# Loads and stores of whole activations cut by blocks of 128 rows rather than by groups of 32 partitions, in a two-layer graph network kernel

## The chip, the cores and the metric

The kernel runs on one core of one Trainium2 chip. Its time is the device time of one execution in microseconds (us); the median of three runs is what counts.

## The reference

There are B = 32 graphs of N = 512 nodes with F = 512 features, all in 32-bit floats. Two layers run one after the other, each on a normalized, rectified copy of the activations x:

```python
def reference(x, adj, nodemask, L0_gnn_W, L1_gnn_Wqk, L1_gnn_Wv):
    # layer 0
    h = jnp.maximum(_layernorm(x, axis=-1), 0.0)
    deg = jnp.sum(adj, axis=-1, keepdims=True)
    agg = jnp.einsum('bij,bjf->bif', adj, h) / jnp.maximum(deg, EPS)
    cat = jnp.concatenate([h, agg], axis=2)
    x = x + jax.nn.relu(jnp.einsum('bnf,of->bno', cat, L0_gnn_W))
    # layer 1
    h = jnp.maximum(_layernorm(x, axis=-1), 0.0)
    q, k = jnp.split(h @ L1_gnn_Wqk, 2, axis=-1)
    v = h @ L1_gnn_Wv
    agg = jnp.einsum('bij,bjd->bid', adj, k * mask[:, :, None])
    w = inv_scale * mask * jnp.einsum('bid,bid->bi', q, agg)
    return x + jax.nn.softmax(w, axis=1)[:, :, None] * v
```

(The two layers are written out in one function here; `mask` is nodemask, all ones in the data given, `inv_scale` is 1/sqrt(512), `EPS` 1e-6.)

## The kernel before

One graph is one batch of the loop (`for i in range(1, B)`, L1071 and after; batch 0 is in `start()`). Four matrix products are made for each batch, and each is cut into 2 by 2 blocks and made with seven block products instead of eight (`product`, L112, whose instructions all carry the line of `block_product`, L103). They run on TensorE in a fixed order: `layer1_tv(i - 1)` (tiles ptv, L470), `layer1_u(i)` (pp_u, pr_u, pq_u), `layer0_y(i + 1)` (pp_y and so on), `layer0_out(i + 1)` (pp_o and so on, fourteen block products). So the work of neighbouring batches is interleaved.

The order on every engine is written out by hand (`tc.manual_schedule`). While a product runs, a `Plan` says after which of its block products each other step is issued; `run` (L165) carries it out. So every engine's queue has a fixed order, and an instruction that waits holds up what stands behind it on the same engine. Nearly all DMAs are issued from SyncE (SP); GpSimd issues the ones that add dx onto the result (`add_x1`, L694), and ScalarE issues a few at the start and at the end.

Rows of a graph are laid out in SBUF in a permuted way. A row number is read as q, c, r with Q = 4 values of q, C = 4 values of c and R = 32 values of r, in that order, `row = 128 q + 32 c + r`. Row (q, c, r) stands in partition `32 q + r`, in chunk c of the free dimension. A tile [128, 4, 512] holds a graph's 512 rows of 512 floats, 2 KB each, in this way. This serves the transposition: the tile is written to a scratch buffer in DRAM (dhT, daT, dh1T; L309, L347, L382), read back by `exchange` (L206; tiles shT, saT, sh1T, 512-byte pieces), and turned in 32 by 32 blocks by VectorE (`turn`, L281).

These transfers go between DRAM and tiles in the permuted layout:

- `half_rows` (L202) loads half of a graph, two of the four chunks, into a tile of the pool "n" (two buffers, shared by both uses): x for the first normalization (`FrontH.load`, tile n; "late" for batch 1), and adj (`FrontA.load`, tile a). At the start it loads x of batch 0 into xu from two queues.
- `load_rows` (L193) loads a whole graph: x a second time for the residual sum (`load_x`, L232, tile xu, two buffers), and once the weight Wv (tile wvN).
- `store` (L714) writes half of a finished graph from tile tv, and `store_block` (L708) a quarter of the last one from tile out, alternating between the queues of SP and ScalarE.

All of them go through `by_rows` (L188): it makes four views of the DRAM side, one for each q, each with r outermost (32), then c, then the 512 floats. Each of these moves to or from 32 partitions. From the second pass of the main loop on they are placed so: the half loads of adj at step 12 of layer0_out and step 1 of layer1_tv, those of x at step 6 of layer1_u and step 0 of layer0_y, `load_x` at step 1 of layer0_y, and the stores at steps 9 and 11 of layer0_out. Between them SP issues the unchanged transfers: the scratch writes and reads above, dx (a copy of x after layer 0, 1 MB, L371), and seven tiles w of weights for each batch (`Stream.load`, L415, four buffers).

Of the kernel before, what the change touches and what calls it, by code (L numbers as in the profile page):

```python
# [22 lines left out]
def kernel(  # L23
# [11 lines left out]
    nc = tc.nc  # L35
    B, N, F = x.shape
    C = N // P
    H = F // 2
    Q = 4
    R = 32  # L40
# [144 lines left out]
        def at(self, n, f, *args):  # L185
            self.setdefault(n, []).append(lambda: f(*args))

    def by_rows(src):  # L188

        t = src.rearrange("(q c r) f -> q r c f", q=Q, c=C)  # L190
        return [t[q] for q in range(Q)]

    def load_rows(t, src):  # L193
        for q, rows in enumerate(by_rows(src)):
            nc.sync.dma_start(out=t[q * R:(q + 1) * R, :, :], in_=rows)

    def half_tile(name):
        return big.tile([P, 2, 512], F32, tag="n", bufs=2, name=name)
# [1 line left out]
    one_queue, two_queues = (nc.sync, nc.sync), (nc.sync, nc.scalar)  # L200

    def half_rows(t, src, h, queues=one_queue):  # L202
        for q, rows in enumerate(by_rows(src)):
            queues[q % 2].dma_start(out=t[q * R:(q + 1) * R, :, :], in_=rows[:, 2 * h:2 * h + 2, :])

    def exchange(src, name, t=None, queues=one_queue):  # L206

# [24 lines left out]
    def load_x(b):  # L232
        room_x(b)
        load_rows(X[b], x[b])
# [55 lines left out]
    class FrontH:  # L290
# [8 lines left out]
        def load(self, h, t=None):  # L299
            self.n[h] = half_tile(f"n_{self.b}_{h}") if t is None else t  # L300
            half_rows(self.n[h], x[self.b], h)
# [15 lines left out]
    class FrontA:  # L317
# [9 lines left out]
        def load(self, h):  # L327
            self.n[h] = half_tile(f"a_{self.b}_{h}")
            half_rows(self.n[h], adj[self.b], h)
# [298 lines left out]
    class Post:  # L628
# [77 lines left out]
                )  # L706

        def store_block(self, r, c):  # L708
            for q, dst in enumerate(by_rows(out[self.b])):
                (nc.scalar if q % 2 else nc.sync).dma_start(  # L710
                    out=dst[:, 2 * r:2 * r + 2, ts(c, H)], in_=self.o[q * R:(q + 1) * R, 2 * r:2 * r + 2, ts(c, H)]
                )

        def store(self, h):  # L714
            v = self.half(h).rearrange("p (c f) -> p c f", c=2)
            for q, dst in enumerate(by_rows(out[self.b])):
                nc.sync.dma_start(out=dst[:, 2 * h:2 * h + 2, :], in_=v[q * R:(q + 1) * R])


    wide = const.tile([P, 14, 2, H], F32, name="wide")  # L720
# [57 lines left out]
    def start():  # L778
# [24 lines left out]
        for h in range(2):  # L803
            half_rows(X[0][:, 2 * h:2 * h + 2, :], x[0], h, two_queues)
# [81 lines left out]
        nc.sync.dma_start(out=mask_sb, in_=nodemask)  # L886
        wvN = xu_tile("wvN").rearrange("p (c f) -> p c f", c=C)
        load_rows(wvN, wv)
        r2, l0 = right_sums(of(w2R)), left_sums(of(h0))

# [177 lines left out]
    with tc.manual_schedule(engines=engines):  # L1068
        weights, mvR = start()
        post = None  # L1070
        for i in range(1, B):  # L1071
            more, last = i + 1 < B, i + 1 == B
            f = F1[i] = FrontH1(i)
# [240 lines left out]
```

## Time and profile before

| | |
|---|---|
| median of 3 runs (lowest to highest) | 2264.93 us (2263.68 to 2269.67) |
| the profiled execution | 2263.74 us |
| span of its trace, first to last instruction | 2262.0 us |
| granted TensorE clock in it | 1.000 |
| HBM read, written | 293.93 MB, 167.51 MB |

One execution is profiled. "Busy" is the time in which an engine has an instruction running. The page gives busy times by engine, the span in 40 slices (busy tenths; for DMA the mean share of the core's 16 DMA engines, and GB/s), the DMA queues with the time that their packets took as a share of 16 engines, and the chain of work that ended last. The DMA list gives, for each line of the program that issues transfers, how many, how large, and how long from issue to landing (the median). The changed ones and their main neighbours, in the kernel before:

| transfer | issues | KB each | us to landing |
|---|---|---|---|
| a<-in_adj_dram | 256 | 128 | 3.0 |
| n<-in_x_dram | 240 | 128 | 3.7 |
| late<-in_x_dram | 8 | 128 | 8.3 |
| xu<-in_x_dram (load_x) | 124 | 256 | 5.4 |
| xu<-in_x_dram (start, 4 on SP, 4 on ScalarE) | 8 | 128 | 4.7 |
| wvN<-in_L_gnn_Wv_dram | 4 | 256 | 6.0 |
| out_dram<-tv | 248 | 128 | 3.4 |
| out_dram<-out (8 on SP, 8 on ScalarE) | 16 | 64 | 1.7 and 2.0 |
| w<-dw (unchanged) | 217 | 256 | 4.2 |
| dh1T<-h1m, sh1T<-dh1T (unchanged) | 124, 256 | 256, 128 | 3.2, 3.4 |
| dhT<-n, shT<-dhT (unchanged) | 120, 248 | 256, 128 | 2.7, 6.0 |
| daT<-a, saT<-daT (unchanged) | 124, 240 | 256, 128 | 3.0, 3.3 |
| tv<-dx, from GpSimd (unchanged) | 62 | 512 | 8.6 |

### The profile page before, as it was taken

Reading aid. Unit: us, or ns where it says so; the run is one execution under the profiler, and the core shown is the slowest. Engines: PE = TensorE matmul, PEld = TensorE weight load, DVE = VectorE, ACT = ScalarE, POOL = GpSimd, SP = SyncE. Lnnn points to the kernel's source line nnn. Section 1 sums busy time; section 2 is a strip of 40 time slices with the busy share of each in tenths; the row PEclk is TensorE's granted clock in tenths of the full one; section 3 lists DMA queues with packets and bytes.
Section 4 is the critical chain, followed back from the end, with each engine's and each line's share of the span. In section 5 each row is a group of like instructions: output and inputs, shape, how many; then the busy total and the mean of one; then the engine's idle time right before and its main releaser. Section 6 shows DMA issues by size and latency. Waiting matters only on the chain.

```text
span 2262.0 us, 32862 instructions
## 1 busy us (share of the span) xinstructions
PE 2253.7 (100%) x10526; PEld 1981.3 (88%) x10526; DVE 1913.5 (85%) x3778; ACT 1024.9 (45%) x1895; POOL 175.6 (8%) x261
## 2 busy tenths in 40 slices
PE   9999999999999999999999999999999999999999
PEld 7888888888888888888888888888888888888888
DVE  7988888888888888888888888888888888888776
ACT  4454443445434544434454344543444443445323
POOL 0010000000000000000000000000000000000000
PEclk9999999999999999999999999999999999999999
DMA  9988787888877887877878788888778777887644
GB/s 205 252 233 246 208 208 193 205 222 219 209 200 192 212 227 204 207 198 201 233 207 209 198 199 218 221 205 203 194 211 228 203 208 193 205 231 209 156 120 108
DMA packets 409997, 463.69 MB, mean 205 GB/s; under 512 B 38208, under 2 KB 271680, under 8 KB 405600
## 3 DMA queue, kind: packets, MB, share of 16 engines
q1 hardware_dynamic: 396608, 426.46, 69.3%
q0 software_dynamic: 8928, 32.51, 8.8%
q10 hardware_dynamic: 4288, 2.62, 0.6%
q8 instruction: 83, 1.36, 0.3%
q14 instruction: 90, 0.74, 0.1%
HBM read 293.93 MB, written 167.51 MB: 204 GB/s over the span
## 4 chain that ended last, share of the span: by engine, by line
PE 98%; DMA 1%; SPq 0%; ACT 0%; issue 0%; DVE 0%; DVEq 0%
PE ptv L470 28%; PE pp_o L103 19%; PE pp_y L103 10%; PE pp_u L103 10%; PE pq_o L103 9%; PE pq_y L103 5%; PE pq_u L103 5%; PE pr_o L103 5%; PE pr_y L103 2%; PE pr_u L103 2%; PE pw L521 1%; DMA mv<-in_L_gnn_Wqk_dram 0%; PE pp_v L103 0%; PE pp_t L103 0%; DMA w<-dw 0%; DMA xu<-in_x_dram 0%
## 5 line engine op out<-in xcount | busy, mean ns | idle before, releaser
L470 PE MATMUL ptv<-mv,h1T 128*128 128x256 f32 x2842 | 618.4, 379 | 0.0
L470 PEld LDWEIGHTS ptv<-mv,h1T 128*128 128x128 f32 x2842 | 539.9, 190 | 73.7 <-DVE xu L449 0.4
L74 DVE TENSOR_TENSOR tv<-tv 128x256 f32<-128x256 f32 (+1 forms) x645 | 322.0, 511 | 13.2 <-ACT tv L80 1.5
L80 ACT ACTIVATE tv<-ptv 128x512 f32<-128x512 f32 (+1 forms) x360 | 185.0, 541 | 262.9 <-PE ptv L470 261.9
L103 PE MATMUL pp_u<-h1m,aT 128*128 128x256 f32 x1024 | 241.9, 379 | 0.0
L103 PE MATMUL pp_y<-wide 128*128 128x256 f32 x992 | 234.4, 379 | 0.7 <-ACT y L80 0.7
L103 PE MATMUL pp_o<-y,aT 128*128 128x256 f32 x992 | 234.3, 379 | 0.0
L103 PE MATMUL pp_o<-w,wide 128*128 128x256 f32 x960 | 226.8, 379 | 0.0
L103 PEld LDWEIGHTS pp_u<-h1m,aT 128*128 128x128 f32 x1024 | 194.5, 190 | 26.4
L103 PEld LDWEIGHTS pp_y<-wide 128*128 128x128 f32 x992 | 188.3, 190 | 26.6 <-ACT y L80 1.1
L103 PEld LDWEIGHTS pp_o<-y,aT 128*128 128x128 f32 x992 | 188.4, 190 | 25.6
L103 PEld LDWEIGHTS pp_o<-w,wide 128*128 128x128 f32 x960 | 182.4, 190 | 24.8
L80 ACT ACTIVATE o<-pp_o 128x512 f32<-128x512 f32 x96 | 57.3, 597 | 300.1 <-PE pp_o L103 300.1
L80 ACT ACTIVATE y<-pp_y 128x512 f32<-128x512 f32 x124 | 74.0, 597 | 234.0 <-PE pp_y L103 234.0
L74 DVE TENSOR_TENSOR tv<-ptv,tv 128x512 f32<-128x512 f32 x240 | 139.9, 615 | 43.2 <-PE ptv L470 39.6
L80 ACT ACTIVATE xu<-pp_u 128x512 f32<-128x512 f32 x127 | 75.8, 597 | 193.6 <-PE pp_u L103 193.6
L77 DVE TENSOR_TENSOR h1T<-h1T 128x512 f32<-128x512 f32 (+1 forms) x183 | 158.3, 879 | 1.2
L251 POOL TENSOR_TENSOR rstd<-rstd,mhalf 128x2 f32<-128x2 f32 (+1 forms) x97 | 79.8, 823 | 642.5 <-DVE rstd L250 642.5
L103 PE MATMUL pq_u<-h1m,aT 128*128 128x256 f32 x512 | 121.0, 379 | 0.0
L74 DVE TENSOR_TENSOR tv<-ptv,m_tv 128x512 f32<-128x512 f32 (+1 forms) x120 | 72.1, 623 | 56.6 <-PE ptv L470 55.4
L103 PE MATMUL pq_y<-wide 128*128 128x256 f32 x496 | 117.3, 379 | 0.0
L103 PE MATMUL pq_o<-y,aT 128*128 128x256 f32 x496 | 117.2, 379 | 0.0
(173 smaller groups left out, 3354.7 us busy)
## 6 DMA issues: line engine op xcount, KB each, us to landing
w<-dw SPq DMA_DIRECT2D x217, 256.0 KB, 4.2
a<-in_adj_dram SPq DMA_DIRECT2D x256, 128.0 KB, 3.0
dx<-xu SPq DMA_DIRECT2D x32, 1024.0 KB, 5.0
sh1T<-dh1T SPq DMA_DIRECT2D x256, 128.0 KB, 3.4
shT<-dhT SPq DMA_DIRECT2D x248, 128.0 KB, 6.0
daT<-a SPq DMA_DIRECT2D x124, 256.0 KB, 3.0
xu<-in_x_dram SPq DMA_DIRECT2D x124, 256.0 KB, 5.4
dh1T<-h1m SPq DMA_DIRECT2D x124, 256.0 KB, 3.2
```

Source lines behind the costliest of these rows:

```text
L74: (on or nc.vector).tensor_tensor(o, a, b, op=ALU.add)
L77: (on or nc.vector).tensor_tensor(o, a, b, op=ALU.subtract)
L80: nc.scalar.activation(o, i, AF.Copy)
L103: nc.tensor.matmul(p[:, rc, :], lt[:, LEFT[k], dk, ts(rc, P)], right[:, dk, :], start=first and rc == 0 and dk == 0, stop=True, skip_group ...
L251: nc.gpsimd.tensor_tensor(rstd[:, a:b], rstd[:, a:b], mhalf[:, a:b], op=ALU.pow)
L470: nc.tensor.matmul(banks[n][:, :, ts(i, P)], left[:, LEFT[k], LEFT_IN[j], :], mvR[:, RIGHT[k], RIGHT[j], :, :], start=first and i == 0, st ...
L521: nc.tensor.matmul(banks[n][:, ts(i, P)], left[:, LEFT[k], LEFT_IN[j], :], mvR[:, RIGHT[k], RIGHT[j], which, :], start=first and i == 0, s ...
```

## The change

The four views of a DRAM tensor are cut by chunk c rather than by q. One transfer then moves one chunk, [128 partitions, 512 floats], between all 128 partitions and the DRAM rows (q, r) of this c: four blocks of 32 rows, 64 KB each, 256 KB apart. On the SBUF side its access pattern is partitions (128), then floats; on the DRAM side it is q (4), then r (32), then floats. A half load or a store of half a graph becomes two transfers of 256 KB where it was four of 128 KB; a load of a whole graph stays four of 256 KB. `four` returns its argument. The sequence of steps is the same on every engine; no compute instruction changes.

```diff
-    def by_rows(src):
-
-        t = src.rearrange("(q c r) f -> q r c f", q=Q, c=C)
-        return [t[q] for q in range(Q)]
+    def by_chunk(src):
+
+        t = src.rearrange("(q c r) f -> c q r f", q=Q, c=C)
+        return [t[c] for c in range(C)]
+
+    def four(v):
+        return v
 
     def load_rows(t, src):
-        for q, rows in enumerate(by_rows(src)):
-            nc.sync.dma_start(out=t[q * R:(q + 1) * R, :, :], in_=rows)
+        for c, rows in enumerate(by_chunk(src)):
+            nc.sync.dma_start(out=four(t[:, c, :]), in_=rows)
...
     def half_rows(t, src, h, queues=one_queue):
-        for q, rows in enumerate(by_rows(src)):
-            queues[q % 2].dma_start(out=t[q * R:(q + 1) * R, :, :], in_=rows[:, 2 * h:2 * h + 2, :])
+        for c, rows in enumerate(by_chunk(src)[2 * h:2 * h + 2]):
+            queues[c].dma_start(out=four(t[:, c, :]), in_=rows)
...
         def store_block(self, r, c):
-            for q, dst in enumerate(by_rows(out[self.b])):
-                (nc.scalar if q % 2 else nc.sync).dma_start(
-                    out=dst[:, 2 * r:2 * r + 2, ts(c, H)], in_=self.o[q * R:(q + 1) * R, 2 * r:2 * r + 2, ts(c, H)]
+            for a, dst in enumerate(by_chunk(out[self.b])[2 * r:2 * r + 2]):
+                (nc.scalar if a else nc.sync).dma_start(
+                    out=dst[:, :, ts(c, H)], in_=four(self.o[:, 2 * r + a, ts(c, H)])
                 )
 
         def store(self, h):
             v = self.half(h).rearrange("p (c f) -> p c f", c=2)
-            for q, dst in enumerate(by_rows(out[self.b])):
-                nc.sync.dma_start(out=dst[:, 2 * h:2 * h + 2, :], in_=v[q * R:(q + 1) * R])
+            for c, dst in enumerate(by_chunk(out[self.b])[2 * h:2 * h + 2]):
+                nc.sync.dma_start(out=dst, in_=four(v[:, c, :]))
```

## The prediction, made before the changed kernel was run

> **What bounds the kernel now.** I read the page from the top: busy shares, slices, DMA queues, chain.
>
> ```profile
> PE 2253.7 (100%) x10526; PEld 1981.3 (88%) x10526; DVE 1913.5 (85%) x3778; ACT 1024.9 (45%) x1895; POOL 175.6 (8%) x261
> ...
> DMA  9988787888877887877878788888778777887644
> GB/s 205 252 233 246 208 208 193 205 222 219 209 200 192 212 227 204 207 198 201 233 207 209 198 199 218 221 205 203 194 211 228 203 208 193 205 231 209 156 120 108
> DMA packets 409997, 463.69 MB, mean 205 GB/s; under 512 B 38208, under 2 KB 271680, under 8 KB 405600
> ...
> q1 hardware_dynamic: 396608, 426.46, 69.3%
> q0 software_dynamic: 8928, 32.51, 8.8%
> ...
> PE 98%; DMA 1%; SPq 0%; ACT 0%; issue 0%; DVE 0%; DVEq 0%
> ```
>
> TensorE sets the end: 2253.7 of 2262.0 us, and 98% of the chain. Only 8.3 us of the span have PE idle, so that is about the most a better transfer can win. But the DMA engines are no idle bystander: the queues' shares add up to 69.3 + 8.8 + 0.6 + 0.3 + 0.1 = 79.1% of sixteen engines. There is cover for a fifth more DMA work, if it is spread evenly, and not for more.
>
> Next the chain in order of time gives the beat of one batch, and the timeline of SP's queue shows where the changed transfers stand in it.
>
> ```profile
> 1086.94 21.15 PE ptv L470 x98
> ...
> 1132.27 3.45 PE pp_o L103 x16
> ...
> 1156.44 3.67 PE ptv L470 x17
> ```
> ```profile
> 1117.64 4.94 SPq L204 DMA_DIRECT2D n<-in_x_dram  x8
> 1122.68 1.79 SPq L195 DMA_DIRECT2D xu<-in_x_dram  x4
> 1125.61 1.79 SPq L212 DMA_DIRECT2D shT<-dhT  x4
> 1134.03 3.79 SPq L415 DMA_DIRECT2D w<-dw  x2
> ...
> 1145.32 1.74 SPq L717 DMA_DIRECT2D out_dram<-tv  x4
> ```
>
> One batch takes 1156.44 - 1086.94 = 69.50 us. In it SP issues, in one order, the four changed megabytes (half loads L204 of adj and of x, load L195 of x, stores L717) among the unchanged ones.
>
> Last, the stretches table (columns: stretch, length, busy time of each engine, clock, DMA share, GB/s) in two stretches each of two batches: the first and third lie in `w<-dw`, which fills 128 partitions, the others in `xu<-in_x_dram`, 32 partitions to a transfer.
>
> ```profile
> 619.00:621.00 2.00, 2.00 (x11) 1.76 (x10) 1.97 (x4) 1.25 (x3) 0.00 (x0) 1.00 1.02 376
> 637.00:639.00 2.00, 2.00 (x11) 1.77 (x10) 1.75 (x2) 0.09 (x1) 0.00 (x0) 1.00 1.04 255
> 688.50:690.50 2.00, 2.00 (x11) 1.75 (x10) 1.97 (x4) 1.25 (x3) 0.00 (x0) 1.00 1.02 380
> 706.50:708.50 2.00, 2.00 (x11) 1.77 (x10) 1.75 (x2) 0.09 (x1) 0.00 (x0) 1.00 1.01 253
> ```
>
> With all engines taken, 128-partition transfers move 376/16/1.02 = 23.0 GB/s an engine, 32-partition ones 255/16/1.04 = 15.3. This is what the change could win.
>
> **Part 1: fewer, wider transfers.** By the list of DMA issues the changed ones are a 256, n 240, xu 124 and 8, late 8, wvN 4, out 248 and 16: 904 issues, 134.2 MB, or 4.19 MB a batch. After it there are 516 (half loads and stores halve, load_x keeps four). SP spends 1.74/4 = 0.435 us on an issue, so 388 x 0.435 = 169 us of SP are saved, worth 0: SP is not on the chain (0%), and its long waits are on PE and ACT. No compute instruction is added or moved. A chunk's consumer now waits for one transfer instead of for four quarters; that is worth 0 too, because PE already runs without a gap.
>
> **Part 2: the packets.** They stay 2 KB. If all sixteen engines still share each transfer, the 4.19 MB cost 4.19/16/23.0 = 11.4 us an engine instead of 17.1: 5.7 us a batch less DMA, hidden behind PE.
>
> **Part 3: how a transfer is dealt out.** Before, the outermost count is 32 or 128 on both sides of every transfer. Now SBUF has 128 partitions, but DRAM is written as q (4) by r (32) by f: its outermost count is four. No row of the trace has such a transfer, so I bound: it is shared by sixteen engines (as in the `w<-dw` rows, whose share of 1.02 is of sixteen engines), or by four, one for each q block, and then whether these are the same four each time is open as well. I take four, always the same: the diff changes just this count, equal shares cut along it can't be more than four, and I see nothing that would rotate them.
>
> [...]
>
> **The sum for four engines**, per batch, on the four:
> - changed transfers: 4.19/4 = 1.05 MB an engine. At 23.0 GB/s 45.6 us, at 15.3 68.5. I take 45.6: the destination fills 128 partitions as in `w<-dw`.
> - the rest, still on all sixteen: 79.1% of 2262 over 32 batches is 55.9 us; less the changed ones' present 4.19/16/15.3 = 17.1 leaves 38.8. If the rest too ran at 23.0, its (463.69 - 134.2)/32 = 10.3 MB would take 28.0: the lower bound.
> - together 84.4 us against PE's 69.5. PE's cover is used up; the excess is 14.9 us a batch.
>
> Two small terms I set against each other: relief of the rest from 32-partition crowding (0 to 10.8 us) and idle moments of the four, chiefly where SP waits for dh1T before it may read it back (dh1T lands in 3.2 us, of which its bytes are 256 KB/16/23.0 = 0.7; some 2.5 us a batch).
>
> At the start, x of batch 0 is on the chain (xu<-in_x_dram, 4.82 us). On four engines its 1.05 MB takes 11.4, +6.6; adj of batch 0 follows on the same four, +6.6 by the same price: 13.
>
> Sum: 2262.0 + 30 batches x 14.9 = 447, + 13 = 2722; with the 1.7 us around the span (2263.74 - 2262.0) 2724. The median of the runs shown is 2264.93, 1.2 above the profiled execution: nothing beside the rest.
>
> Where it is late first: n and xu, 2.1 MB issued at 1117.64, keep the four busy for 2.1/4/23.0 = 22.8 us, to 1140.4. The read of shT and the w tiles of 1134.03 queue behind them: half a megabyte of shT in small packets (0.52 MB/16/11.5, the price of rival 4's row, 2.8 us), 0.7 for a w tile, and some 2.5 of landing make 1146.4. That w is due in the ninth of the fourteen block products of layer0_out, at 1132.27 + 8 x 1.73 = 1146.1 (half of a 3.45 us piece each). One batch just passes, but stores (11.4 us from 1145.32) and the adj halves follow at once, and the backlog of the next batch starts 15 us deeper. Then PE waits for w and, through VectorE, for X and for the tiles that VectorE turns: sh1T's turn stands in VectorE's queue ahead of the u sums that PE's banks wait for.
>
> **Rivals.**
> 1. *Sixteen engines all the same* (not slower). Place: every changed transfer; price: part 2, 5.7 us a batch less DMA behind PE; only the start's 4.82 us load shrinks, by up to a third: 2262 to 2266, say 2263. For it: equal bytes, 2 KB packets, 128 partitions. Against: the outermost four. It decides as soon as the shares on an engine stay under 69.5 us a batch, that is from 4.19/k/23.0 + 38.8 < 69.5, k of 6 engines upward.
> 2. *Four engines, but others each time.* The load stays even; a 256 KB transfer takes 256 KB/4/23.0 = 2.8 us rather than 0.7, covered by the many microseconds between issue and use; only the start pays, 5 us: 2270. Against: something must rotate them.
> 3. *Four engines, crowded.* The moved packets keep the 15.3 GB/s: 68.5 + 38.8 = 107.3 a batch, 2262 + 30 x 37.8 + 13 = 3409; with half of that extra price 3070. For it: four streams of 64 KB blocks now compete with sixteen-wide traffic on the same engines, and SP's waits in order leave holes. Against: 12 engines are less busy meanwhile.
> 4. *No slowdown of the rest at all*: 45.6 + 28.0 = 73.6 a batch, 2262 + 123 + 13 = 2400. Against: 271680 of the 409997 packets are under 2 KB, and from 639 to 646 us, where these prevail (1136 of 1446), the DMA lines give 166 GB/s at 90.6%, 11.5 an engine.
>
> **How the numbers follow.** Four fixed engines at about the sum 0.72, crowded (3) 0.11, rest relieved (4) 0.05, sixteen (1) 0.08, rotating (2) 0.04. The forecast is the likeliest: 2724. Cases 3 and 4 bound the unknown price; the range reaches halfway into each, 2450 to 3070, and leaves out the not-slower cases and the far tails, 0.2 together. A change of 0.3% (6.8 us) is about what a measurement of this kernel tells from none. Slower: 0.72 + 0.11 + 0.05 = 0.88. Cases 1 and 2 hold the rest, 0.05 faster (start and 32-partition crowding both gone) and 0.07 within.
>
> **What would show it.** In the profile after: PE's share about 2254/2724 = 83%, with its idle time ended by DMA or by VectorE waiting for DMA; mean rate 463.69 MB/2724 us = 170 GB/s; mean DMA share near (45.6 x 4 + 38.8 x 16)/16/84.4 = 59% although the transfers are the bound (four full, twelve at 38.8/84.4 = 46%); w<-dw, unchanged in itself, landing well above its 4.2 us; a, n, xu above 5. A beat of some 84 us between two tv stretches. I am wrong if the DMA slices stay at 7 or 8 tenths with landing times as now (rival 1), or if landings of the changed transfers double while w's stay at 4 and PE stays at 99% (rival 2). A beat over 95 us with moved packets at 15 GB/s would be rival 3.

## The result, and the profile after

The changed kernel takes 2798.09 us (median of 5 runs, 2795.69 to 2802.97) against 2264.44 us before: a ratio of 1.2354, 95% interval 1.2337 to 1.2371. It is slower by 534 us. Its profiled execution spans 2793.6 us.

The page of the changed kernel, the same lines as those shown of before:

```profile
PE 2413.4 (86%) x10526; PEld 2070.9 (74%) x10526; DVE 1914.7 (69%) x3778; ACT 1013.7 (36%) x1895; POOL 177.9 (6%) x261
...
DMA  4655665655656556656566565566565665655653
GB/s 121 209 158 161 166 179 166 176 158 162 183 167 180 160 164 173 178 166 180 154 167 177 169 178 159 167 172 178 167 182 153 167 177 171 172 154 169 173 136 88
DMA packets 397589, 463.57 MB, mean 166 GB/s; under 512 B 25808, under 2 KB 259280, under 8 KB 393200
...
q1 hardware_dynamic: 384376, 426.41, 50.4%
q0 software_dynamic: 8928, 32.51, 6.5%
...
PE 46%; DMA 39%; ACT 9%; DVE 2%; issue 2%; SPq 1%; ACTq 0%; POOL 0%; DVEq 0%; POOLq 0%
```

The same bytes move, and their packets take less time in all (the queues' shares sum to 57.6% of a longer span, 1609 us an engine against 1789), yet the kernel is slower and DMA now holds 39% of the chain. A mean over sixteen engines hides this: it falls while the transfers become the bound. Stretches of the changed kernel show why (columns: stretch, length, busy times, granted clock, DMA share, GB/s):

```profile
1332.00:1344.00 12.00, 12.00 (x58) 10.55 (x57) 10.36 (x18) 2.90 (x6) 0.39 (x1) 1.00 0.27 102
1344.00:1346.00 2.00, 2.00 (x11) 1.77 (x10) 1.97 (x4) 0.52 (x2) 0.34 (x1) 1.00 0.62 180
1346.00:1347.00 1.00, 1.00 (x6) 0.88 (x5) 1.00 (x2) 1.00 (x3) 0.00 (x0) 1.00 0.30 101
1276.00:1279.00 3.00, 3.00 (x7) 2.46 (x8) 0.00 (x0) 0.00 (x0) 0.00 (x0) 0.50 0.37 107
1279.00:1281.00 2.00, 2.00 (x9) 1.67 (x9) 0.00 (x0) 0.00 (x0) 0.00 (x0) 0.85 0.27 101
1315.00:1319.00 4.00, 4.00 (x10) 3.16 (x10) 3.90 (x10) 2.90 (x8) 0.00 (x0) 0.50 1.02 225
1319.00:1322.00 3.00, 3.00 (x12) 2.45 (x11) 2.90 (x8) 1.29 (x3) 0.00 (x0) 0.74 1.03 382
```

In the first row only loads of x are under way, several of them in the queue at once, and the share stands at 0.27 of sixteen for 12 us: a little over four engines, 102/4 = 25.5 GB/s each. That several transfers together still fill only four says that they are the same four each time, unless the queue moved one transfer at a time on changing engines. The next two rows speak against that: the 2.1 MB of x issued from 1327.23 on last at 102 GB/s until about 1348, and in the middle of them reads of shT run on further engines (0.62), after which x goes on alone as before (0.30 at 101 GB/s). (The clock column of the other rows is used below.)

The chain of the changed kernel in order of time, one batch:

```profile
1259.98 2.27 PE pr_o L103 x11
1262.25 13.61 DMA w<-dw
1275.86 0.14 issue
1275.99 5.48 PE pp_o L103 x16
...
1284.54 8.09 DMA dhT<-n
1292.64 5.37 DMA a<-in_adj_dram
...
1298.17 0.41 ACT a L336
...
1304.13 7.75 DMA dh1T<-h1m
...
1312.61 0.62 ACT h1m L388
...
1313.25 0.69 DVE h1m L77
1313.94 0.61 DVE tv L74
...
1314.69 3.75 PE pp_u L103 x8
1318.44 2.83 PE pr_u L103 x8
1321.27 1.73 PE pp_u L103 x8
```

The transfers on it are w, dhT and dh1T, none of which was changed, and a, which was. They are late because of the load on the four engines: the extra writes below, in the same form and with nobody waiting for them, cost 315 us, and the same bytes with 128 rows outermost nothing. TensorE's timeline of the same batch (start, length, line, and in brackets the idle time before and what ended it) shows where it loses time:

```profile
1268.45 1.89 PE L103 MATMUL pq_o<-y,aT 128*128 128x256 f32 x8
1275.99 3.74 PE L103 MATMUL pp_o<-w,wide 128*128 128x256 f32 x8 [5.65 <-DMA w<-dw]
...
1281.30 1.89 PE L103 MATMUL pq_o<-w,wide 128*128 128x256 f32 x8
...
1288.20 21.32 PE L473 MATMUL ptv<-mv,h1T 128*128 128x256 f32 x98
1314.69 3.75 PE L103 MATMUL pp_u<-h1m,aT 128*128 128x256 f32 x8 [5.17 <-DVE tv L74]
1318.23 3.04 PE L103 MATMUL pr_u<-h1m,aT 128*128 128x256 f32 x8
1321.11 1.89 PE L103 MATMUL pp_u<-h1m,aT 128*128 128x256 f32 x8
```

There are two places. In layer0_out, TensorE waits 5.65 us for a w tile, at the ninth block product. At the start of layer1_u it waits 5.17 us for VectorE; the chain above leads from there through VectorE (L77, L74) and ScalarE's masking of h1m to the landing of dh1T, and before that through ScalarE's sum of adj to the landing of a. After each wait the next matmuls are slow: eight take 3.74 and 3.75 us instead of 1.89, and after the second wait eight more take 3.04. In the clock column above the granted clock is 0.50 there, against 1.00 in the first row. Counted from start to start, where eight matmuls are 1.73 us apart and a ptv stretch takes 21.15: the wait on w costs 1275.99 - 1268.45 - 1.73 = 5.81, the slow ones behind it 1281.30 - 1275.99 - 2 x 1.73 = 1.85, the second wait 1314.69 - 1288.20 - 21.15 = 5.34, and its slow ones 1321.11 - 1314.69 - 2 x 1.73 = 2.96: together 15.96 us. By TensorE's timeline one batch takes 85.5 us (median distance of two starts of ptv) against 69.5: 16.0.

The whole account, by the starts of the first and the last ptv stretch (113.6 and 2129.3 us before, 161.9 and 2649.3 after): 48.3 us lost up to the first, 471.7 in the 29 batches between, 11.6 behind the last. Together 531.6, the difference of the two spans.

### The profile page after: what moved, and what is told of

It is laid out like the page before. It is cut to its first block, busy times and chain, and to the rows that moved or that the text cites. A ratio compares the mean times of both kernels' runs of the same rounds, so it can differ in the third digit from the quotient of the medians.

```text
span 2793.6 us, 32123 instructions
## 1 busy us (share of the span) xinstructions
PE 2413.4 (86%) x10526; PEld 2070.9 (74%) x10526; DVE 1914.7 (69%) x3778; ACT 1013.7 (36%) x1895; POOL 177.9 (6%) x261
## 4 chain that ended last, share of the span: by engine, by line
PE 46%; DMA 39%; ACT 9%; DVE 2%; issue 2%; SPq 1%; ACTq 0%; POOL 0%; DVEq 0%; POOLq 0%
DMA w<-dw 13%; PE pp_o L103 11%; PE pp_u L103 10%; DMA dh1T<-h1m 8%; DMA dhT<-n 8%; PE pp_y L103 8%; DMA a<-in_adj_dram 5%; PE pq_y L103 4%; PE pq_u L103 4%; PE pr_o L103 3%; PE pr_u L103 3%; ACT n L264 2%; ACT tv L80 2%; PE pr_y L103 2%; ACT a L336 2%
## 5 line engine op out<-in xcount | busy, mean ns | idle before, releaser
L103 PE MATMUL pp_u<-h1m,aT 128*128 128x256 f32 x1024 | 293.6, 438 | 145.8 <-DVE tv L74 137.3
L103 PE MATMUL pp_o<-w,wide 128*128 128x256 f32 x960 | 276.8, 440 | 163.0 <-DMA w<-dw 163.0
L103 PEld LDWEIGHTS pp_u<-h1m,aT 128*128 128x128 f32 x1024 | 222.7, 221 | 193.6 <-ACT a L336 146.8
L103 PEld LDWEIGHTS pp_o<-w,wide 128*128 128x128 f32 x960 | 209.4, 222 | 207.8 <-issue 173.8
L74 DVE TENSOR_TENSOR tv<-tv 128x256 f32<-128x256 f32 (+1 forms) x645 | 321.6, 510 | 13.2 <-ACT tv L80 1.5
L77 DVE TENSOR_TENSOR h1m<-h1m 128x512 f32<-128x512 f32 x128 | 85.3, 687 | 214.9 <-ACT h1m L388 213.7
L80 ACT ACTIVATE tv<-ptv 128x512 f32<-128x512 f32 (+1 forms) x360 | 174.4, 536 | 150.9 <-PE ptv L473 150.9
L103 PEld LDWEIGHTS pp_o<-y,aT 128*128 128x128 f32 x992 | 197.6, 199 | 30.7
L74 DVE TENSOR_TENSOR o<-m_o,o 128x512 f32<-128x512 f32 x32 | 22.2, 692 | 219.7 <-ACT o L80 219.6
L74 DVE TENSOR_TENSOR tv<-ptv,tv 128x512 f32<-128x512 f32 x240 | 137.1, 612 | 39.8 <-PE ptv L473 39.6
L77 DVE TENSOR_TENSOR h1T<-h1T 128x512 f32<-128x512 f32 (+1 forms) x183 | 158.1, 877 | 1.2
L388 ACT ACTIVATE h1m<-h1m,mraw 128x512 f32<-128x512 f32 x124 | 85.0, 710 | 194.0 <-DMA dh1T<-h1m 194.0
L336 ACT ACTIVATE a<-a 128x512 f32<-128x512 f32 x128 | 79.8, 624 | 182.7 <-DMA a<-in_adj_dram 167.0
```

The costliest lines, as they stand in the source:

```text
L74: (on or nc.vector).tensor_tensor(o, a, b, op=ALU.add)
L77: (on or nc.vector).tensor_tensor(o, a, b, op=ALU.subtract)
L80: nc.scalar.activation(o, i, AF.Copy)
L103: nc.tensor.matmul(p[:, rc, :], lt[:, LEFT[k], dk, ts(rc, P)], right[:, dk, :], start=first and rc == 0 and dk == 0, stop=True, skip_group ...
L336: nc.scalar.activation(v, v, AF.Copy, accum_out=DEG[self.b][:, c:c + 1])
L388: nc.scalar.activation(self.rows(c), self.raw[c], AF.Copy, scale=mraw[:, c, self.b:self.b + 1])
```

## The experiments

Three theories were set against each other. A: a transfer runs on as many engines as its outermost DRAM count allows, always the same ones, and the sum of work on the fullest engines sets the beat. B: the new form is slow for another reason, its width or its scattered blocks. C: no engine is full, but each new transfer takes longer to land, and whoever needs it waits. A fourth, D, came up on the way: what counts is the backlog on the four engines when some transfer is due. Beats are medians of the distance between two starts of ptv in TensorE's timeline. All kernels were measured against the kernel before on the same chip.

### Other outermost counts: 16, 8 and 2 blocks

```diff
-        t = src.rearrange("(q c r) f -> c q r f", q=Q, c=C)
+        t = src.rearrange("(q c r) f -> c q r f", q=16, c=C)
```

and the same with q=8 and q=2.

> The changed transfers keep 128 partitions and one chunk each, but the DRAM side is 16 blocks of 8 rows instead of 4 blocks of 32 (other rows of the same graph stand in each partition, so the output is not the reference's). Theory A (a transfer is dealt to as many engines as its outermost DRAM count allows, always the same ones, and the fullest engines set the beat): 4.19/16/23.0 = 11.4 us plus 38.8 for the rest, 50.2 against PE's 69.5 a batch: hidden, 2257 to 2266 us. Theory B (width or scattered DRAM blocks as such are slow, the count has nothing to do with it): about 2790. Theory C (no engine is full; PE waits for single landings, which four-engine transfers make longer): also about 2262, so this run parts B from A and C.

Measured: 2262.78 us, ratio 0.9995 (0.9986 to 1.0004), beat 69.5.

> The same with 8 blocks of 16 rows (other rows again, output not the reference's). A: 4.19/8/23.0 = 22.8 plus 38.8 = 61.6 a batch, under 69.5: hidden in the main loop, with at most some 10 us at the start: 2262 to 2275. C: a 256 KB transfer takes 1.4 us on eight engines, 0.7 on sixteen, 2.8 on four, so a third of the 532 us lost with four stays: about 2440.

Measured: 2285.8 us, ratio 1.0096 (1.008 to 1.0111), beat 69.5. The first ptv starts 12 us late and two more batches take 74; after that nothing is lost. A's start was 10 us too good; C's 2440 is far off.

> The same with 2 blocks of 64 rows (other rows again, output not the reference's). A: 4.19/2/23.0 = 91.1 plus 38.8 = 129.9 a batch, 60.4 above PE's, times 29, plus some 125 at the start and 40 at the end: about 4180. C: a landing of 5.7 us in place of 2.8 stretches the 532 us to about 1270: 3530. The DMA share in a stretch with only these transfers should be 2/16 = 0.13 at some 50 GB/s under A.

Measured: 3976.16 us (one run), beat 122.9. A stretch of this kernel with only such transfers:

```profile
1065.00:1075.00 10.00, 10.00 (x48) 8.80 (x47) 9.82 (x18) 4.09 (x7) 1.62 (x2) 1.00 0.13 50
```

Two of sixteen engines, 25 GB/s each, as A said; its 4180 was 204 us too high, and C's 3530 446 too low. The three kernels and the changed one move the same bytes in the same number of transfers with the same 128 partitions; only the outermost count differs, and with it the size of the blocks in DRAM. The size alone is not what costs: in the control of the extra writes below each transfer is one whole block of 256 KB with 128 rows outermost, and it costs nothing (these are writes; loads of this form were not run). So the count is the cause, and B is out. The run with 16 also answers what full width is worth where it is not spoilt, by the page of that kernel:

```profile
PE 2253.0 (100%) x10526; PEld 1981.6 (88%) x10526; DVE 1913.7 (85%) x3778; ACT 1025.1 (45%) x1895; POOL 174.9 (8%) x261
...
DMA  9989777777777787777877777777778777787544
```

The DMA digits are a tenth lower in many slices than before, and the time is the same within its interval: TensorE covers all of it. By the queues' shares on the two pages (79.1% before, 66.8 + 8.7 + 0.5 + 0.3 + 0.1 = 76.4% here) the wide form saves 1.9 us of DMA a batch, not the 5.7 of the prediction. A stretch of loads of x in this kernel shows a reason, 299/16/1.04 = 18.0 GB/s an engine where the prediction took 23.0:

```profile
636.00:637.00 1.00, 1.00 (x6) 0.90 (x5) 0.56 (x1) 0.00 (x0) 0.00 (x0) 1.00 1.04 299
```

### Only the start

```diff
+    wide_now = {"now": {"n", "a", "xu", "out"}}
...
         weights, mvR = start()
+        wide_now["now"] = set()
```

(`load_rows`, `half_rows` and the stores take the old form for the kinds that are not in the set.)

> Only the transfers that batch 0 and the set-up issue before the main loop are in the new form (7 MB: x of batches 0, 1, 2, adj of 0 and 1, Wv, the second load of x of batch 1); the main loop and the last stores have the old one. The prediction gave the start 13 us: 2275. If the start is bound by the same sum (DMA share before 0.96 of 113.6 us, less 30 for the 7.34 MB at 15.3 GB/s on sixteen, plus 7.34/4/23.0 = 79.8 on four, 159 us instead of 113.6), it is 2297 to 2310.

Measured: 2308.87 us, ratio 1.0197 (1.0183 to 1.0211): 44.6 us lost. The start's cost is that of the sum, not the 13 us of the prediction.

### Parts of the change in the main loop

```diff
+        wide_now["now"] = {"n", "xu"}
...
+        wide_now["now"] = {"a", "out"}
...
+        wide_now["now"] = {"n", "a", "xu"}
...
+        wide_now["now"] = {"out"}
```

(one line in each of four kernels; their starts have the old form)

> In the main loop alone, and there only for the two loads of x (half loads and load_x), the new form; adj, stores and the start in the old one. Theory A: two of the four changed megabytes on four engines, 2.1/4/23.0 = 22.8, plus the rest 38.8 and the other two at 8.6, 70.2 us a batch against 69.5: 2262 to 2300. Theory C (each landing adds its share of the loss): half of the 472 us that the main loop lost: about 2500.

Measured: 2476.68 us, ratio 1.0941 (1.0917 to 1.0964), beat 77.1.

> The other two alone, in the main loop: the half loads of adj and the stores in the new form, x in the old. A: the same sum, 70.2 us a batch: 2262 to 2300, as in the run with x alone, since it is bytes on the four engines that count and not which transfer. C: the two runs differ by whichever landing PE waits for, and add up to 472 us: here 0 to 472 over 2264.

Measured: 2548.37 us, ratio 1.1257 (1.124 to 1.1274), beat 78.5.

> In the main loop the loads of x (both) and adj in the new form, the stores in the old. A: 3.15/4/23.0 = 34.2, plus 38.8 and 4.3 for the stores, 77.3 us a batch, 7.8 over PE's, times 29: about 2490. C: three quarters of 472: 2616, or the sum of the losses of the run with x alone and of adj's part.

Measured: 2618.99 us, ratio 1.1569 (1.1552 to 1.1586), beat 81.6.

> In the main loop and at the end only the stores of the result in the new form. The sum is 11.4 + 38.8 + 12.8 = 63.0 us a batch, under 69.5. A: hidden, 2262 to 2270. D: each half's store keeps the four engines for 5.7 us instead of some 2, and the writes of dhT, the loads of adj that wait for them and the writes of dh1T stand behind; some of the 284 us of the run with adj and stores stay: 2300 to 2450.

Measured: 2296.27 us, ratio 1.0144 (1.0129 to 1.0159), beat 70.0; between the two forecasts, below D's.

A failed in all four: sums under or just over 69.5 do not hide, and the third kernel, with a sum of 77.3, came out 129 us above A's 2490. C's number for the run without the stores was hit to 3 us and for x alone to 23, but C had failed with 8 and with 2 blocks. What the pairs share with the changed kernel is the place of the wait. The waits of TensorE (what it waited for: us in total, times, longest), with x alone:

```profile
PE pp_o L103 <- DMA w<-dw: 139.4, 28, 5.7
```

and with adj and stores alone:

```profile
PE pp_u L103 <- DVE tv L74: 135.6, 28, 5.4
```

In the changed kernel both stand, the second in the same size, the first longer:

```profile
PE pp_o L103 <- DMA w<-dw: 170.1, 29, 8.7
PE pp_u L103 <- DVE tv L74: 137.3, 29, 5.9
```

The loads of x make w late, adj and the stores together make dhT, adj, dh1T and so layer1_u late. It takes the stores, and they do not do it alone: with x and adj but without the stores the wait at layer1_u is 18.3 us and the one on w 237.3, and with the stores alone TensorE has no such wait at layer1_u and 1.7 us on w. Adj alone was not run. The losses of the two runs, 212 and 284 us, add up to 497, against 483 that the changed kernel loses behind its start.

### Extra writes that nobody waits for

```diff
+    def extra(b):
+
+        d = dram.tile([512, 512], F32, tag="extra", name=f"extra_{b}_{len(extras)}")
+        extras.append(d)
+        v = d.rearrange("(q c r) f -> c q r f", q=Q, c=C)
+        for c in range(C):
+            nc.sync.dma_start(out=v[c], in_=w2R[:, c, :, :].rearrange("p b f -> p (b f)"))
...
+                p.at(11, extra, i)
...
+                p.at(5, extra, i)
```

added to the kernel before, in the plans of layer1_tv and layer1_u; in the control the view is `d.rearrange("(c p) f -> c p f", c=C)`.

> The kernel before, with two extra writes of 1 MB a batch (from batch 1 to 29) of a constant tile to a scratch buffer that nobody reads, each as four transfers of [128, 512] with the DRAM side in 4 blocks of 32 rows. No step of the kernel waits for them. A: 55.9 us a batch of DMA now, plus 2.1/4/23.0 = 22.8 on the four: 78.7, 9.2 over PE's, times 29: about 2530. C: nobody waits for them, so 2262 to 2275.

Measured: 2579.41 us, ratio 1.1376 (1.135 to 1.1402), beat 80.9.

> The control of the run with extra writes: the same 2 MB a batch to a scratch buffer that nobody reads, issued at the same places, but with the DRAM side as 128 rows outermost. A and D alike: 2.1/16/23.0 = 5.7 us more on each engine, 61.6 a batch: 2262 to 2275. If extra bytes or extra issues on SP were what cost time there, it would be near the 2579 of that run.

Measured: 2263.24 us, ratio 0.9998 (0.9988 to 1.0007), beat 69.5.

C is out: no step of the program waits for these writes, and they cost 315 us, 49 more than A's 2530, while the same bytes and issues spread over sixteen engines cost nothing. The harm is done in the queue, to others: TensorE waits 241.4 us for w, and in the list of SP's waits the pauses before other issues (L204, L212, L347) that end with the landing of such a write sum to 160.6 + 134.0 + 18.2 = 312.8 us.

### The same bytes, less of them ahead of w

```diff
-                p.at(1, load_x, i + 1)
+                p.at(1, load_x_part, i + 1, 0)
...
                 p.at(2 * n + 1, stream.load)
+                if n == 1 and i > 1:
+                    p.at(3, load_x_part, i, 1)
```

`load_x_part(b, h)` loads chunks 2h and 2h + 1 of x. Made once with x alone in the new form, once with the whole change.

> As the run with x alone in the new form (2477), but only chunks 0 and 1 of the second load of x are issued before the w tiles, chunks 2 and 3 behind the second of them. Bytes, and so the sum per batch (70.2 us on the four engines), are the same; what is queued ahead of w falls from 2.1 MB on four engines (22.8 us) to 1.57 MB (17.1 us). Theory A (the sum on the fullest engines, with a fixed share of holes, sets the beat): no change, 2460 to 2490. Theory D (what counts is the backlog on the four engines at the moment when a transfer is due; PE waits there some 5 us a batch and runs slowly for some 2 us behind the wait): the wait on w nearly goes, 2270 to 2330.

Measured: 2367.33 us, ratio 1.0449 (1.0433 to 1.0465), beat 72.3. The order alone is worth 109 us, which A excludes; D expected more. TensorE's waits for w in this kernel:

```profile
PE pp_o L103 <- DMA w<-dw: 72.7, 29, 5.7
```

Half of the wait is left, but at another place. None of the 29 waits is at the ninth block product any more; all are at the thirteenth, for the last w tile of the batch, which is now issued behind the two chunks that were moved. The chain of one batch shows it, with the last two block products between the landing of w and ptv:

```profile
1265.89 3.45 PE pp_o L103 x16
1269.34 0.07 PE pq_o L103
1269.42 12.22 DMA w<-dw
...
1281.77 3.69 PE pp_o L103 x16
1285.46 4.75 PE ptv L493 x22
```

All but two of these waits last 2.0 to 3.4 us, and behind 19 of the 29 the next eight matmuls run at full speed. The mean granted clock is 0.992, against 0.969 with x alone. So TensorE's waiting for w falls by 67 us and its busy time by 42 (from 2322.6 to 2280.4): together the 109. D's reading of the ninth product held; it did not see that what is moved makes the next tile late.

> The changed kernel with the same split of the second load of x. A: the four engines have 84.4 us of work a batch whatever the order, so the beat can't fall below that: 2760 to 2800, no gain. D without A's floor: the wait on w (170 us of PE in all, and the slow matmuls behind it) goes, about 2590 to 2620.

Measured: 2732.51 us, ratio 1.2065 (1.2044 to 1.2086), beat 83.1. That is 66 us less than the changed kernel and lies in neither forecast: 27 us under A's 2760 to 2800, 112 over D's 2590 to 2620. The waits of this kernel:

```profile
PE pp_u L103 <- DVE tv L74: 132.3, 29, 5.5
PE pp_o L103 <- DMA w<-dw: 85.1, 31, 7.5
PE ptv L478 <- ACT tv L80: 53.5, 28, 4.2
```

The wait on w halves, and part of what it gives comes back as a wait on ScalarE in layer1_tv: with the four engines nearly full, what is taken from one place seems to be late at the next. The beat lies below the prediction's 84.4, so that sum can't be a floor as it stands.

### What the runs say together

With the measured 25.5 GB/s in place of 23.0 for the new transfers, and the prediction's other terms (38.8 us for the rest, 17.1/4 = 4.3 for each of the four megabytes left in the old form, 55.9 for the whole kernel before), the work on the fullest engines and the beat are:

| kernel | work on the fullest engines, us a batch | beat, us |
|---|---|---|
| 16 blocks | 10.3 + 38.8 = 49.1 | 69.5 |
| 8 blocks | 20.6 + 38.8 = 59.4 | 69.5 |
| stores alone | 10.3 + 38.8 + 12.8 = 61.9 | 70.0 |
| x alone | 20.6 + 38.8 + 8.6 = 68.0 | 77.1 |
| x alone, split | 68.0 | 72.3 |
| adj and stores | 68.0 | 78.5 |
| all but the stores | 30.8 + 38.8 + 4.3 = 73.9 | 81.6 |
| extra writes | 55.9 + 20.6 = 76.5 | 80.9 |
| the change, split | 41.1 + 38.8 = 79.9 | 83.1 |
| the change | 79.9 | 85.5 |
| 2 blocks | 82.2 + 38.8 = 121.0 | 122.9 |

The 25.5 was measured with loads on four and, nearly so, on two engines; for 8 and 16 engines and for writes it is an estimate, too good for 16: by its page (76.4% of 2260.7 us over 32 batches) that kernel has 54.0 us of work a batch, not 49.1. Within this the work is a floor that no run goes under. How far above it, or above TensorE's 69.5, a kernel lies depends on the backlog ahead of what is due (the split moves it by 4.8 and by 2.4 us at equal work). By and large the distance is smaller where the work is larger, and with two engines it is 1.9 us. No version beat the kernel before, and by its 8.3 us of idle TensorE none could by much; a form with 128 partitions that keeps the kernel's own order of rows and yet has an outermost count of 16 was not tried.

## Why the prediction came out as it did

**What bounds before** held: with sixteen engines the saving of DMA time was invisible (0.9995), so all of the result comes from part 3. The saving was mis-sized, 1.9 us a batch and not 5.7, which cost the forecast nothing.

**Four engines, the same ones each time** held: the share of 0.27 at 102 GB/s shows it, and that of 0.13 at 50 GB/s with two; the beats of 69.5 with 8 and 16 fit it. When the prediction chose four, no run had shown how such a transfer is dealt out; it was the author's estimate, from the count that the diff changes. Which of the sixteen engines they are no view here shows. The 128 partitions in one transfer did not help here: with 16 blocks, which have them too, the ratio is 0.9995, and the views that give them take the 32 away from the outermost place on the DRAM side.

**The sum for four engines**, 84.4 us a batch, met the beat of 85.5, but two of its terms were off and nearly made up for each other. The price of 23.0 GB/s, taken from the w rows, should have been 25.5: 41.1 us, not 45.6. And the two terms set against each other did not cancel: the beat lies 5.6 us above the corrected work of 79.9. (The prediction divided its prices by the share as well. So read, the new price is 102/16/0.27 = 23.6 and the work 83.2, 2.3 under the beat; but the same reading puts the kernel with two blocks, at 50/16/0.13 = 24.0, on 126.1, above its beat of 122.9.) Moments in which the engines stand idle while SP waits in order do show: before it may load adj, SP waits for dhT to land (360.5 us in all, 12.4 a batch), and behind one such wait nothing moves for a microsecond:

```profile
1293.00:1294.00 1.00, 1.00 (x6) 0.90 (x5) 0.84 (x4) 0.43 (x1) 0.00 (x0) 1.00 0.00 0
```

That such moments add up to the 5.6 us is argued, not counted. Over the 29 beats the excess makes 472 us where 447 were forecast, for 30.

**The start** was the step that failed by most: 13 us were forecast, 48.3 are lost up to the first ptv, 44.6 in the run where only the start has the new form. The prediction looked at the two first loads on the chain and gave everything else of the start the cover of the main loop. The stretch from 0 to 113.6 us of before has a DMA share of 0.96: no cover at all. The sum, applied there (0.96 x 113.6 - 30 + 7.34/4/23.0 = 159 us), gives the 45. There is some luck in it: with 25.5 in place of 23.0 it is 151, so something else at the start takes 8 us, and no run shows what. The end's 11.6 us were not in the sum at all. With the main loop's 25, the start's 35 and the end's 12, 72 us, the 2724 becomes 2796, the time of the profiled execution (2795.69).

**Where it is late first** was right on the first place, w in the ninth block product. For the second it had VectorE's tiles, in the end rightly, but by another road: not the turn of sh1T, but ScalarE's queue, where the sum of adj and the masking of h1m wait and hold up what TensorE needs.

**Left out**: TensorE's slow restart, 1.85 + 2.96 = 4.8 of the 16.0 us of a batch. Over 29 batches that is 139 of the 160 us by which PE's busy time, 2413.4, exceeds the 2253.7 that were put into the forecast share of 83%; it came out at 86%. Here waits of 5.65 and 5.17 us were followed by a granted clock of 0.50 for some 3 and 5 us. Of the shorter waits some have this cost and some do not. One of 2.85 us in the start-only run was followed by eight matmuls in 3.78 us, twice the 1.89 of full speed. In the changed kernel one of 2.17 us was followed by eight in 2.91 us and eight more in 2.68, while the granted clock went to 0.50, and behind one of 2.59 us eight took 1.99 at 1.00 (timeline, and stretches with the columns of above):

```profile
198.24 1.99 PE L103 MATMUL pq_u<-h1m,aT 128*128 128x256 f32 x8 [2.59 <-ACT m_u L80]
...
247.90 2.91 PE L103 MATMUL pp_o<-w,wide 128*128 128x256 f32 x8 [2.17 <-DMA w<-dw]
250.60 2.68 PE L103 MATMUL pp_o<-y,aT 128*128 128x256 f32 x8
```
```profile
247.90:249.50 1.60, 1.60 (x6) 1.35 (x7) 0.00 (x0) 0.00 (x0) 0.00 (x0) 0.77 0.46 142
249.50:250.80 1.30, 1.30 (x5) 1.02 (x4) 0.00 (x0) 0.00 (x0) 0.00 (x0) 0.50 0.43 133
250.80:252.00 1.20, 1.20 (x5) 0.92 (x4) 0.88 (x2) 0.00 (x0) 0.00 (x0) 0.50 0.32 114
198.24:200.20 1.96, 1.96 (x8) 1.43 (x8) 1.55 (x6) 0.51 (x1) 0.00 (x0) 1.00 0.25 94
```

By these runs no length of a single wait parts the two cases.

**Rivals.** Crowding (3) did not come: the moved packets ran faster than assumed, not at 15.3 GB/s. Relief of the rest (4) did not come either: the changed kernel's shares make 57.6% of 2793.6 us, 50.3 a batch, and less 41.1 x 0.27 = 11.1 for the moved packets they leave 39.2 for the rest, against 38.8 before. Sixteen (1) and rotating engines (2) are excluded by the share of 0.27 with several transfers under way.

## What to carry to other kernels

Before reshaping a transfer, write down the outermost count of its access pattern in DRAM, not only the partitions: here 4 in place of 32 put 134 MB onto a quarter of the engines (a share of 0.27). Then add up the work of the fullest engine for each stage, the start by itself, and compare it with what covers it; a mean DMA share of 58% did not show that four of sixteen were nearly full. Staying under the cover is needed but not enough: a burst of slow transfers in SP's queue made whatever stood behind it late, here even with 68 us of work in a beat of 69.5 (it became 77.1 with x alone), and a wait can cost more than its length where TensorE restarts slowly behind it, here behind waits of some 5 us (the one of 5.65 cost 1.85 more) and behind some of 2 to 3.

## What was not expected

The issue of a transfer itself slows down when the four engines have a backlog. SP's queue in the changed kernel:

```profile
1331.93 9.12 SPq L198 DMA_DIRECT2D xu<-in_x_dram  x4
1341.14 5.76 SPq L215 DMA_DIRECT2D shT<-dhT  x4
1347.01 8.66 SPq L418 DMA_DIRECT2D w<-dw  x2
```

The same four issues of xu took 1.79 us before. In the changed kernel's list for L198 the median issue takes 2.172 us, and four in 9.12 us are 2.28 each, near the 256 KB/4/25.5 = 2.6 us in which the four engines move one such transfer: SP goes on at about the pace at which they empty. So w, which fills all sixteen (a share of 1.02 in its stretches before), is held up twice: first it can't be issued (two issues took 8.66 us here, 3.79 before), then its part on the four engines waits; the second half of this follows from the backlog and is not seen by itself. Why an issue is held no view here shows.
